# A two-layer graph attention kernel: the sums of W one step later, less background work in three panels, and a bias added by DMA

## The chip, the cores and the metric

The kernel runs on one core of one Trainium2 chip. The metric is the device time of one execution in microseconds (us). Most executions of one kernel lie within 0.3% of each other. Of the kernel before, three runs were known at the start: median 3235.16 us (3231.14 to 3235.99). Every comparison below has its own runs of the kernel before, made on the same chip in the same rounds.

## The reference

There are 2708 rows of 1024 features in float32, and a 0/1 adjacency matrix. Two layers, cut to what matters:

```
# layer 0
h = relu(layernorm(x))
f, g = h @ Wf + bf, h @ Wg + bg
attention = softmax(where(adj > 0, relu(f @ g.T), -9e15), axis=1)
x = x + attention @ (h @ W + bW)
# layer 1
h = relu(layernorm(x)) @ W1
e = leaky_relu(h @ a1 + (h @ a2).T)
x = x + relu(softmax(where(adj > 0, e, -9e15)) @ h)
```

The rows of a softmax sum to one, so `attention @ (h @ W + bW)` is `(attention @ h) @ W + bW`. The kernel uses this form: the bias bW is simply added to the rows of x to which the projected result is added.

## The kernel before

Layer 0 works on five column panels (0 to 4) of the attention matrix, two of 586 columns and three of 512. For each panel there are four stages on TensorE: the scores, the q of the next panel, the aggregate of this panel with h, and the projection with W. All large products are done as seven half-size products, called M1 to M7; the sums that this method needs run on VectorE, GpSimd and ScalarE. Layer 1 follows.

Three parts matter. First, background work. Pieces with an estimated cost in VectorE time are queued, and after a product the code hands out credit for some of them. The loads that a piece needs are issued when it is one of the next two:

```python
def one():
    for it in later[:2]:
        if it[1]:
            it[1]()                    # the loads of this piece
            it[1] = None
    us, _, go = later.pop(0)[:3]
    go()
    return us

def behind(us, psum_free=False):
    credit[0] = min(credit[0] + us, 2 * us)
    while later and credit[0] > 0 and (psum_free or not later[0][3]) and (not later[0][4] or later[0][4]()):
        credit[0] -= one()
```

In the scores, `behind(rate)` follows the products, with `rate = 0.6 if p == 0 else 1.0`. In an aggregate the rate is 3.0.

Second, the sums of the quarters of W (of both layers). `prepare_W` queues eight pieces. Each loads two tiles of 512 KB of W's rows from the stream pool, which has 12 tiles and is shared with `hc`, the rows of h that the aggregate streams in:

```python
def prepare_W():
    def fetch(l, k):
        ...
        rows[l, k] = [load_rows(w_in[l], c, "w_rows") for c in (k, k + NH)]
    def go(l, k):
        two = rows.pop((l, k))
        ...                            # layer 1: dot products with a1, a2
        right_of_W(l, k, *two)         # sums on VectorE, four stores
    for l in range(2):
        for k in range(NH):
            put(2.7 if l == 0 else 8.0, lambda l=l, k=k: go(l, k), lambda l=l, k=k: fetch(l, k))
```

It is called just ahead of the aggregate of panel 0. Third, the rows to which the projection adds:

```python
def finish0(p):
    bwb = [slot(f"bwb{e}") for e in range(2)]
    ...                                # bwb: the bias in every partition
    def start(ts):
        for t in ts:
            ...
            for e in range(2):
                load(xs[t][e], x[r0:r0 + n, e * W:(e + 1) * W])
                nc.gpsimd.tensor_add(xs[t][e], xs[t][e], bwb[e][:n, :W])
```

## Time and profile before

| | kernel before |
|---|---|
| time, median | 3235.16 us |
| span of the profiled run | 3235.3 us |
| TensorE busy | 3137.1 us (97%) |
| TensorE idle (difference) | 98.2 us |
| VectorE busy | 1756.3 us (54%) |
| GpSimd busy | 395.0 us (12%) |
| moved by DMA | 641.43 MB |

How to read it: with TensorE at 97%, the question isn't which engine is the bottleneck. It is where TensorE's 98.2 us of idle time lie, and where its busy time is long because the granted clock is low. The prediction shows the lines for this: the list of TensorE's waits, then the timeline of each stage.

### The profile page before, as it was taken

To read this page: it belongs to the slowest core of one execution; us is meant where nothing else is said; L and a number is where in the kernel's file an instruction comes from. 1 tells how busy PE (TensorE), PEld (TensorE's weight loads), DVE (VectorE), ACT (ScalarE), POOL (GpSimd) and SP (SyncE) were. 2 spreads that over 40 slices of the span, in tenths; PEclk is the share of its full clock that TensorE was granted. 3 is DMA by queue.
4 is the path that set the end of the run, shared out by engine and by line. 5 is a ranking of instruction groups with operands and counts; after the bars stand their busy time and mean duration, and the time that the engine had idled before them with its cause. 6 is when DMAs were issued, how large, how long until landed. Compare 5 with 4: busy or idle time off the path is not lost. (4 is left out here: it accounts for less than half of the span.)

```text
span 3235.3 us, 35363 instructions
## 1 busy us (share of the span) xinstructions
PE 3137.1 (97%) x12924; PEld 2333.4 (72%) x12924; DVE 1756.3 (54%) x3594; ACT 507.7 (16%) x853; POOL 395.0 (12%) x476
## 2 busy tenths in 40 slices
PE   8999999999999999999999998997999999999998
PEld 5577767667876578876888885864767748778585
DVE  7857594275812766327581358537574272553712
ACT  4412120010200102001020002003131030211200
POOL 3723110210002100021000101020010000000001
PEclk9999999999999999999999999998999999999999
DMA  6958866576445575457745565665555445555546
GB/s 262 332 174 297 276 229 227 171 243 215 141 130 163 173 247 190 151 191 242 228 156 156 165 209 185 225 237 200 198 161 175 148 159 171 186 189 175 194 150 212
DMA packets 279628, 641.43 MB, mean 198 GB/s; under 512 B 50686, under 2 KB 116178, under 8 KB 279456
## 3 DMA queue, kind: packets, MB, share of 16 engines
q1 hardware_dynamic: 245184, 525.56, 50.5%
q0 software_dynamic: 34272, 113.62, 9.4%
q8 instruction: 102, 1.67, 0.2%
q14 instruction: 70, 0.57, 0.1%
HBM read 525.49 MB, written 113.58 MB: 198 GB/s over the span
## 5 line engine op out<-in xcount | busy, mean ns | idle before, releaser
L917 PE MATMUL sz<-B,As 128*128 128x256 f32 (+3 forms) x1320 | 328.9, 399 | 5.3 <-DVE st L44 5.3
L917 PEld LDWEIGHTS sz<-B,As 128*128 128x128 f32 (+1 forms) x1320 | 248.7, 189 | 64.5 <-DVE st L44 6.4
L917 PE MATMUL sx<-B,As 128*128 128x256 f32 (+3 forms) x880 | 227.0, 401 | 14.2 <-DMA As<-hs_d 12.0
L756 POOL TENSOR_TENSOR gT<-gT,rr 128x2048 f32<-128x2048 f32 (+3 forms) x20 | 68.3, 3433 | 1320.5 <-DVE rr L44 700.2
L917 PE MATMUL sy<-B,As 128*128 128x256 f32 (+3 forms) x880 | 219.5, 392 | 0.0
L478 PE MATMUL gy<-T,hc 128*128 128x256 f32 (+3 forms) x880 | 205.7, 395 | 6.6 <-DMA hc<-hg_d 6.6
L478 PE MATMUL gx<-P,hc 128*128 128x256 f32 (+3 forms) x880 | 204.5, 394 | 4.7 <-ACT P L1147 4.7
L478 PE MATMUL gz<-Sa,hc 128*128 128x256 f32 (+3 forms) x880 | 206.6, 394 | 0.0
L478 PE MATMUL gz<-P,hc 128*128 128x256 f32 (+3 forms) x880 | 206.3, 393 | 0.0
L917 PEld LDWEIGHTS sx<-B,As 128*128 128x128 f32 (+1 forms) x880 | 162.3, 189 | 51.4 <-issue 11.2
L478 PEld LDWEIGHTS gy<-T,hc 128*128 128x128 f32 (+1 forms) x880 | 168.5, 192 | 42.3 <-DVE junk L44 4.4
L478 PEld LDWEIGHTS gx<-P,hc 128*128 128x128 f32 (+1 forms) x880 | 168.4, 192 | 40.9 <-ACT P L1147 5.0
L917 PEld LDWEIGHTS sy<-B,As 128*128 128x128 f32 (+1 forms) x880 | 163.9, 186 | 38.2 <-issue 0.9
L478 PEld LDWEIGHTS gz<-Sa,hc 128*128 128x128 f32 (+1 forms) x880 | 165.6, 190 | 31.8
L478 PEld LDWEIGHTS gz<-P,hc 128*128 128x128 f32 (+1 forms) x880 | 165.6, 190 | 31.8
L821 PE MATMUL px<-w,gT 128*128 128x512 f32 x320 | 147.3, 613 | 11.5 <-issue 10.0
L821 PE MATMUL py<-w,ps 128*128 128x512 f32 (+1 forms) x352 | 155.6, 593 | 0.3 <-DVE mcol L44 0.3
L821 PE MATMUL pz<-w,ps 128*128 128x512 f32 (+1 forms) x352 | 155.0, 592 | 0.0
L616 ACT COPY mask<-mk_ps 128x1024 bf16<-128x1024 bf16 (+1 forms) x55 | 55.6, 1011 | 575.8 <-PE mk_ps L615 254.6
L821 PEld LDWEIGHTS pz<-w,ps 128*128 128x128 f32 (+1 forms) x352 | 65.5, 186 | 85.6 <-issue 81.7
L821 PEld LDWEIGHTS py<-w,ps 128*128 128x128 f32 (+1 forms) x352 | 65.4, 186 | 85.6 <-issue 82.7
L821 PEld LDWEIGHTS px<-w,gT 128*128 128x128 f32 x320 | 62.5, 197 | 89.2 <-issue 85.3
(240 smaller groups left out, 4797.9 us busy)
## 6 DMA issues: line engine op xcount, KB each, us to landing
hc<-hg_d SPq DMA_DIRECT2D x350, 512.0 KB
As<-hs_d SPq DMA_DIRECT2D x150, 512.0 KB
w<-wt_d SPq DMA_DIRECT2D x96, 512.0 KB
w<-in_L_gnn_W_dram SPq DMA_DIRECT2D x72, 512.0 KB
md<-md_d SPq DMA_DIRECT2D x56, 512.0 KB
adj_i<-in_adj_dram SPq DMA_DIRECT2D x50, 512.0 KB
hg_d<-g POOLq DMA_DIRECT2D x40, 512.0 KB, 5.0
hs_d<-hsT POOLq DMA_DIRECT2D x40, 512.0 KB, 5.6
```

Source lines behind the costliest of these rows:

```text
L478: nc.tensor.matmul(ps[d], left(m, k, d), right(m, k), start=(start and k == 0), stop=(k == K - 1), skip_group_check=True)
L616: nc.scalar.copy(mk[:n, :, :k4 * P], ps[:n, :, :k4 * P])
L756: nc.gpsimd.tensor_tensor(of(e, s), of(e, s), by(s, k), OP.mult)
L821: nc.tensor.matmul(ps, left[i][m][:, k, :], w_[k], start=(start and k == 0), stop=(k == NH - 1), skip_group_check=True)
L917: nc.tensor.matmul(ps[:n, :h], lefts[q][:, i % 2, c, :n], B[m][c // 2][:, c % 2, :h], start=(start and c == 0), stop=(c == NH - 1), skip_g ...
```

## The change

The intent: let the first products of panel 0's aggregate have the load queue for themselves; let VectorE convert the masks in time, by giving panels 2 to 4 fewer credits per product; and take 44 additions from GpSimd, a row of which holds up one VectorE instruction in the kernel before (8.50 us for 0.69).

```diff
-        rate = 0.6 if p == 0 else 1.0
+        rate = (0.6, 1.0, 0.65, 0.65, 0.65)[p]
 ...
     def finish0(p):
-        bwb = [slot(f"bwb{e}") for e in range(2)]
-        for e in range(2):
-            load(bwb[e][:, :W], bass.AP(tensor=bw.tensor, offset=bw.offset + e * W, ap=[[0, P], [1, W]]))
 ...
                     load(xs[t][e], x[r0:r0 + n, e * W:(e + 1) * W])
-                    nc.gpsimd.tensor_add(xs[t][e], xs[t][e], bwb[e][:n, :W])
+                    nc.gpsimd.dma_start(xs[t][e], bass.AP(tensor=bw.tensor, offset=bw.offset + e * W, ap=[[0, n], [1, W]]),
+                                        accum_op=OP.add)
 ...
-        if p == 0:
-            prepare_W()
-        then = {}
+        then = {M5: prepare_W} if p == 0 else {}
```

`then = {M5: prepare_W}` queues the pieces behind the product M5, the second of the aggregate's seven.

## The prediction

> **What bounds the kernel now.** I read the page first, then the list of waits of TensorE, then its timeline stage by stage.
>
> ```profile
> PE 3137.1 (97%) x12924; PEld 2333.4 (72%) x12924; DVE 1756.3 (54%) x3594; ACT 507.7 (16%) x853; POOL 395.0 (12%) x476
> ```
>
> TensorE is busy 97% of 3235.3 us. The change neither adds nor removes a product, so only its idle 98.2 us, and the time in which it runs below full clock, can be won. The list of TensorE's waits says what it is idle for (total, times, longest):
>
> ```profile
> PE mk_ps L615 <- DVE nm L44: 17.0, 9, 3.4
> PE mx_ps L654 <- DVE mx L44: 14.8, 1, 14.8
> PE sx L917 <- DMA As<-hs_d: 12.0, 4, 4.3
> PE px L821 <- issue: 10.0, 3, 4.8
> PE gy L478 <- DMA hc<-hg_d: 6.6, 2, 4.0
> PE sz L917 <- DVE st L44: 5.3, 2, 4.9
> ```
>
> The 14.8 us (column maximum between the layers) and the 10.0 us lie where the last projection of layer 0 waits on VectorE, ScalarE and stores; the change does not move the order of VectorE there. The other rows are its targets. First, the timeline of TensorE in the first aggregate, with one row of the busy-time-by-stretch view below it (columns: stretch, length, busy PE, PEld, DVE, ACT, POOL, granted clock, DMA share, GB/s):
>
> ```profile
> 446.44 21.87 PE L478 MATMUL gx<-Sa,hc 128*128 128x293 f32 x88
> 470.91 6.26 PE L478 MATMUL gy<-T,hc 128*128 128x293 f32 x24 [2.60 <-DMA hc<-hg_d]
> 481.18 18.81 PE L478 MATMUL gy<-T,hc 128*128 128x293 f32 x64 [4.01 <-DMA hc<-hg_d]
> 499.83 21.87 PE L478 MATMUL gx<-Sb,hc 128*128 128x293 f32 x88
> ```
>
> ```profile
> 468.00:490.00 22.00, 15.39 (x51) 10.83 (x50) 20.07 (x56) 0.66 (x2) 6.49 (x12) 0.84 1.02 401
> ```
>
> A product takes 21.7 us start to start when nothing is late (499.83 to 521.54). The second one, gy, should have started at 446.44 + 21.7 = 468.1 and ended 489.8; it ended 499.8. So 10 us are lost: 6.6 idle and some 3 at half clock after the idle time. The DMA engines are full (share 1.02, 401 GB/s): the sums of W's quarters load 16 tiles of 512 KB and store 32 of 256 KB in this stretch, and their loads stand in the one load queue among those of hc.
>
> Second, a narrow panel's scores (panel 3 of 0 to 4), timeline of TensorE:
>
> ```profile
> 1505.02 1.89 PE L917 MATMUL sx<-B,As 128*128 128x256 f32 x8
> 1510.32 0.66 PE L615 MATMUL mk_ps<-identb,nm 128*74 128x128 bf16 x8 [3.42 <-DVE nm L44]
> 1510.80 3.63 PE L917 MATMUL sz<-B,As 128*128 128x256 f32 x8
> 1514.27 1.89 PE L917 MATMUL sy<-B,As 128*128 128x256 f32 x8
> ```
>
> The transposes of the next mask wait 3.42 us for VectorE to convert it, and the product after them takes 3.63 us for 1.89: half clock. Third, the end of panel 4's scores, all engines:
>
> ```profile
> 1942.98 9.81 POOL L1078 TENSOR_TENSOR x_res<-x_res,bwb 128x512 f32<-128x512 f32 x8
> 1944.85 8.50 DVE L44 SCALAR_TENSOR_TENSOR Sb<-Sb,mask 128x512 f32<-128x512 f32 x1
> 1954.46 3.68 PE L917 MATMUL sz<-B,As 128*128 128x256 f32 x8 [4.93 <-DVE st L44]
> ```
>
> One VectorE instruction that takes 0.69 us at 1962.22 takes 8.50 us here, and ends when GpSimd's eight additions of W's bias end. TensorE then idles 4.93 us and runs its next product at half clock.
>
> **What the skill says.** (1) "SBUF — State Buffer", section "Who interferes with whom": a VectorE instruction with two SBUF inputs contends with a GpSimd instruction that reads SBUF, and the loser is blocked, not slowed. The 8.50 us agree, and show that it can stay blocked through a row of GpSimd instructions. (2) "TensorE: Matmul & The Clock Gate", Part 1: after an idle window the array runs at half clock for about 3.4 us, in windows that run freely. The trace agrees: granted clock 0.50 in 1511 to 1514 and 0.51 in 1955 to 1958. So an idle time of 2 us and more costs up to 1.7 us on top, not every time. (3) "DMA: Bandwidth & Descriptors", section "SWDGE vs HWDGE vs iDMA": an accumulating DMA can only be issued from GpSimd; (4) its section "Queues, rings and completion order" has the DMA engines share their time between queues. That nothing but the queue's turn is lost to the accumulate, no run here shows yet.
>
> **The change part by part.** The order of each engine's instructions in the built kernels was compared; no time is in it.
>
> *Sums of the weights later.* Now all 12 loads of hc of the first two products come before any of W's rows, so gx and gy have their data: -10 us. But W's 16 loads and 32 stores move into the third and fourth product. From 490 to 512 (estimated from the new order of the queue) the engines must move 1 MB of rows of a, 2 MB of W's rows, 4 MB of stores and 5 tiles of hc, about 9.5 MB; at the 401 GB/s seen above that is 23.7 us against 21.7. Some loads of hc also reuse a tile of W's rows, which is free only when its sums have been stored; stores took 6.5 us to land here, which is just in time. I take 3 us idle and 1.5 us of half clock: net -5.5.
>
> *Less background per product.* A product of 8 instructions takes 1.73 us; seven make 12.1, and with the mask's transposes a pair of row blocks is 12.6 us. At rate 1.0 the background may take 7 us of VectorE per pair. Summing the VectorE starts-to-starts of the timeline (0.335 us for 256 columns, 0.605 for 512, 0.72 for a dot product's half, 0.62 for a half of the statistics), the early pairs hold 11.8 to 13.5 us in panel 2 and 12.3 to 14.3 in panel 3, against 12.6. At 0.65 they hold 9.0 to 12.7 and 8.1 to 13.1. What decides is the chain from the end of one pair to the conversion of the next mask, which has five products (8.6 us) where the scheduler has put the transposes early: before, it is 8.2 to 10.8 us, with waits of 0.93 to 3.42. After, four early places are left with a chain of 8.0 to 8.8 us: by the same relation about 1 us each; the two short waits at the start of panel 3 (0.72, 1.19) keep their order and stay. Panel 2: 5.2 idle + 1.7 half clock become about 2.1: -4.8. Panel 3: 6.8 + 1.7 become about 4.2: -4.3. Panel 2 also waits 2.84 us for As, with 3 us of half clock (0.50 in 1160 to 1166), after a burst of mask loads for the background in the same queue; they are spread now, and I count half: -3. Panel 4 has no background work left, so its new rate does nothing. The background's queue ends within the scores at the lower rate too: nothing is pushed into a later stage.
>
> *Bias by DMA.* 44 GpSimd additions of 1.257 us each (some 55 us) go, with 10 bias loads; 44 accumulating DMAs of up to 256 KB come, some 11 MB in all against 641. GpSimd is at 12%, so its own time wins nothing. In four of the five projections the additions run under the last product of the aggregate, where VectorE is idle. Only the fifth collides: -4.93 - 1.7 = -6.6. VectorE's order in that projection also changes: it finishes rows earlier and no longer reaches the evictions late, which cost TensorE 2.74 + 0.75 us and about 1 of clock: -4.5.
>
> Sum: -5.5 - 4.8 - 4.3 - 3 - 6.6 - 4.5 = -28.7. Every reordering of such a schedule opens small waits elsewhere (nine mask waits are there now); I allow +5: -24. 3235 - 24 = 3211.
>
> **Rivals.** (a) *The burst only moves.* The third product starves as the second did: for it, the 9.5 MB above and the tiles that wait for stores; against it, a full product of hc is fetched ahead. Then the first part gives 0: 3217. (b) *The accumulate is slow*: it reads and writes SBUF, and its 2 MB fall into a stretch at 320 GB/s (1942 to 1954), so that the rows come late and VectorE, whose new order has them early, blocks the softmax behind them. Against it, 20 us and more lie between issue and use. It would cost 5 to 10: 3219. (c) *VectorE's waits are set by single long pieces*, not by the rate (a pair's sums are 2.7 us at once), so the masks stay late: the second part gives 3 instead of 12: 3220. (d) All three targets vanish and nothing opens: 3199.
>
> **Range and chances.** The gain is bounded by the identified losses, about 40 us or 1.2%, so 2% (65 us) is out of reach, and nothing added is on TensorE. Times before spread from 3231 to 3236. I take 3200 to 3224; faster by over 2% 0.01, within 2% 0.98, slower 0.01.
>
> **What would show it.** Right: no wait of gy for hc; no VectorE mask-add over 2 us in panel 4 and no wait of sz for st there; waits of mk_ps for nm near 10 us instead of 17.0; no POOL addition of bwb; TensorE's idle time near 80 us. Wrong: a wait of gx or gz for hc between 490 and 530 over 5 us, VectorE or the new DMA as releaser of px or pz, or the mask waits unchanged. A loss over 10 us would mean that the accumulating DMAs hold up the queue of loads.

## The result and the profile after

| | before | after |
|---|---|---|
| time, median of 6 runs | 3233.29 us (3231.14 to 3235.99) | 3210.03 us (3208.94 to 3210.75) |
| span of the profiled run | 3235.3 us | 3207.8 us |
| TensorE busy | 3137.1 us | 3125.8 us |
| TensorE idle (difference) | 98.2 us | 82.0 us |

The ratio is 0.9928, with a 95% interval of 0.9915 to 0.9941. A ratio here is the mean time of one kernel's fast runs over the mean of the other's of the same rounds, so it isn't quite the ratio of the two medians. The kernel became faster by 23 us, within 2%. The prediction was 3211. The two profiled runs exaggerate this: that of before is the slowest of its six (3235.99, 2.7 above the median), that of after lies 0.4 below its median. So the spans differ by 27.5 us and the medians by 23.3, and some 4 us of the stage differences below are chance.

From the profile's page of the kernel after, the busy times, and from its list of TensorE's waits (total, times, longest) the rows that answer to those of before:

```profile
PE 3125.8 (97%) x12924; PEld 2326.2 (73%) x12924; DVE 1747.8 (54%) x3593; ACT 508.5 (16%) x853; POOL 381.3 (12%) x476
...
PE mx_ps L654 <- DVE mx L44: 15.1, 1, 15.1
PE sx L917 <- DMA As<-hs_d: 10.6, 3, 6.0
PE px L821 <- issue: 9.8, 3, 4.6
PE mk_ps L615 <- DVE nm L44: 9.5, 8, 2.5
PE gx L478 <- DMA hc<-hg_d: 6.1, 2, 5.8
PE sx L917 <- DVE sm L44: 2.2, 1, 2.2
```

The reader is to see two things. The same 12924 matmul instructions now take 11.3 us less busy time, which can only be clock or overlap, and TensorE is idle 16.2 us less; the two add up to the 27.5 us between the spans. And of the four target rows, one shrank (mk_ps for nm, 17.0 to 9.5), one is nearly gone (sz for st, 5.3 to 0.7), and one merely has another product's name: gy waited 6.6 us for hc, and now gx waits 6.1. The fourth, sx for As, lost its one wait in panel 2 (2.84 us); the three that are left lie in panel 0's scores, which the change doesn't touch.

Where the time went, stage by stage, is read from TensorE's timelines: each stage runs from the start of its first product to the start of the next stage's first.

| stage (us) | before | after | difference |
|---|---|---|---|
| aggregate of panel 0 | 165.31 | 164.68 | -0.6 |
| scores of panel 1 | 163.87 | 162.28 | -1.6 |
| scores of panel 2 | 151.48 | 139.90 | -11.6 |
| scores of panel 3 | 147.25 | 143.96 | -3.3 |
| scores of panel 4 | 144.82 | 137.94 | -6.9 |
| projection behind it | 55.04 | 48.94 | -6.1 |
| from the last product to the end | 11.02 | 12.86 | +1.8 |

The time up to the aggregate of panel 0 (446.44 and 446.81 us) and each other stage agree within 0.4 us. Up to its last product TensorE thus gained 29.3 us, and the tail took 1.8 back. A stage of unchanged code doesn't take the same time in every execution, so each difference needs that spread beside it. In the traces of this case that lack the change's part for a stage, the aggregate of panel 0 took 164.1 to 166.4 us, the scores of panel 1 163.8 to 165.5, of panel 2 147.1 to 151.5, of panel 3 145.5 to 148.6, of panel 4 144.8 to 146.2, and the projection behind it 53.3 to 55.0. The kernel after lies below all of these ranges except the first.

The aggregate of panel 0 in the kernel after: the timeline of TensorE, then two stretches of the busy-time view (columns as in the prediction):

```profile
446.81 21.87 PE L478 MATMUL gx<-Sa,hc 128*128 128x293 f32 x88
468.52 21.88 PE L478 MATMUL gy<-T,hc 128*128 128x293 f32 x88
490.24 13.98 PE L478 MATMUL gx<-Sb,hc 128*128 128x293 f32 x56
510.03 6.92 PE L478 MATMUL gx<-Sb,hc 128*128 128x293 f32 x16 [5.81 <-DMA hc<-hg_d]
521.27 21.87 PE L478 MATMUL gz<-Sa,hc 128*128 128x293 f32 x88
```

```profile
446.80:490.20 43.40, 43.40 (x177) 33.42 (x176) 19.27 (x45) 2.96 (x6) 0.00 (x0) 1.00 0.47 149
490.20:521.30 31.10, 25.01 (x90) 18.24 (x89) 23.26 (x55) 1.13 (x3) 10.80 (x20) 0.89 0.97 365
```

The first two products are whole now, at full clock and with the DMA engines half used. The third takes 521.27 - 490.24 = 31.0 us instead of 21.7: the full engines, the wait of 5.8 us and the lowered clock (0.89) have moved with the burst by one product.

Panel 3's scores, at the pair that waited 3.42 us before:

```profile
1498.23 0.61 PE L615 MATMUL mk_ps<-identb,nm 128*74 128x128 bf16 x8
1498.67 1.90 PE L917 MATMUL sx<-B,As 128*74 128x256 f32 x8
```

The transposes start without a wait, and the product behind them takes 1.90 us, not 3.63.

The end of panel 4's scores, all engines, and of the view of the accumulating DMAs' line two rows (durations in ns min/median/max, then landing times in us):

```profile
1926.77 6.17 POOL L1075 DMA_DIRECT2D x_res<-in_L_gnn_bW_dram  x7 [0.53 <-DVE sm L44]
1928.13 0.69 DVE L44 SCALAR_TENSOR_TENSOR Sb<-Sb,mask 128x512 f32<-128x512 f32 x1
1936.10 1.89 PE L917 MATMUL sz<-B,As 128*128 128x256 f32 x8
```

```profile
L1075 POOL DMA_DIRECT2D x_res<-in_L_gnn_bW_dram x44: 819/1872/3292, 597.1 to 2114.2; - x44
DMA to landing us min/median/max: 6.3/13.4/21.1
```

The mask addition on VectorE that took 8.50 us takes 0.69 while GpSimd issues the DMAs; sz follows without a wait at full clock. Seven issues take 6.17 us, 0.88 us each. The median of 1.872 us in the second fence isn't the cost of one: the records of neighbouring issues overlap, and the line's busy time is 38.9 us for all 44. Between 1900 and 2010 us TensorE waits for nothing at all, where it waited for st, pt and mcol before (4.9, 2.7 and 0.5 + 0.3 us).

### The profile page after: what moved, and what is told of

Read it like the earlier page. It is cut to its first block, busy times and chain, and to the rows that moved or that the text cites. A ratio compares the mean times of both kernels' runs of the same rounds, so it can differ in the third digit from the quotient of the medians.

```text
span 3207.8 us, 35361 instructions
## 1 busy us (share of the span) xinstructions
PE 3125.8 (97%) x12924; PEld 2326.2 (73%) x12924; DVE 1747.8 (54%) x3593; ACT 508.5 (16%) x853; POOL 381.3 (12%) x476
## 4 chain that ended last, share of the span: by engine, by line
PE 82%; issue 9%; DVE 3%; DMA 3%; POOL 2%; ACT 1%; SPq 0%; POOLq 0%; DVEq 0%; ACTq 0%
PE gy L478 13%; PE gz L478 12%; PE gx L478 12%; PE sz L917 8%; PE sx L917 5%; PE sy L917 5%; PE pz L821 4%; PE M_ps L413 3%; PE qz L478 3%; PE gv L478 3%; PE py L821 3%; PE px L821 3%; PE qy L478 2%; PE qx L478 2%; DMA As<-hs_d 1%
## 5 line engine op out<-in xcount | busy, mean ns | idle before, releaser
L917 PE MATMUL sz<-B,As 128*128 128x256 f32 (+3 forms) x1320 | 321.4, 392 | 0.7 <-DVE st L44 0.7
L478 PEld LDWEIGHTS gz<-Sa,hc 128*128 128x128 f32 (+1 forms) x880 | 165.5, 190 | 31.9
L478 PEld LDWEIGHTS gz<-P,hc 128*128 128x128 f32 (+1 forms) x880 | 165.5, 190 | 31.9
L821 PE MATMUL px<-w,gT 128*128 128x512 f32 x320 | 147.6, 614 | 11.3 <-issue 9.8
```

Source lines behind the costliest of these rows:

```text
L478: nc.tensor.matmul(ps[d], left(m, k, d), right(m, k), start=(start and k == 0), stop=(k == K - 1), skip_group_check=True)
L821: nc.tensor.matmul(ps, left[i][m][:, k, :], w_[k], start=(start and k == 0), stop=(k == NH - 1), skip_group_check=True)
L917: nc.tensor.matmul(ps[:n, :h], lefts[q][:, i % 2, c, :n], B[m][c // 2][:, c % 2, :h], start=(start and c == 0), stop=(c == NH - 1), skip_g ...
```

## The experiments

The kernel before, in the runs of the first four experiments: median 3234.15 us (17 runs). The theory was that each of the three parts acts in its own stages: the sums almost not at all, since the burst only moves; the rates in panels 2 and 3; the bias only in the projection behind panel 4. The main rival was that the bias DMA, by freeing GpSimd and the SBUF access, is what helps the masks too.

### e1_sums: the sums alone

```diff
-        if p == 0:
-            prepare_W()
-        then = {}
+        then = {M5: prepare_W} if p == 0 else {}
```

> The kernel before with only the sums of W queued later. In the trace of the changed kernel the second product of the first aggregate no longer waits for hc, but the third waits 5.8 us instead and runs at half clock after it, so the aggregate as a whole is 0.6 us shorter. Theory (the burst only moved): 0 to -2 us against before, no wait of gy, a wait of gx for hc of 5 to 6 us. Rival (my prediction's step: most of the burst is absorbed by the product fetched ahead, and what the changed kernel shows there comes from the other parts): -5 us or more, wait under 3 us.

Measured: 3231.5 us median of 13 runs, ratio 0.9993 (0.9984 to 1.0001); one of them took 3683.91 us at a granted clock of 0.845; it was slow and is left out of the ratio. The aggregate took 163.61 us, 1.7 less than before, and the third product waits in the place of the second. From TensorE's timeline of this run:

```profile
489.44 13.98 PE L478 MATMUL gx<-Sb,hc 128*128 128x293 f32 x56
508.23 6.87 PE L478 MATMUL gx<-Sb,hc 128*128 128x293 f32 x16 [4.81 <-DMA hc<-hg_d]
```

What follows: rival (a) of the prediction, the burst that only moves, is what happens; the part alone is worth 2.3 us by the ratio, with an interval from 5.2 us down to nothing. Its aggregate, 163.61 us, is only 0.5 us under the fastest one of unchanged code (164.06 in e5_twice).

### e2_rates: the rates alone

```diff
-        rate = 0.6 if p == 0 else 1.0
+        rate = (0.6, 1.0, 0.65, 0.65, 0.65)[p]
```

> The kernel before with only the lower rates in panels 2 to 4. Theory (VectorE's background work between products delays the masks and bursts of mask loads delay As): panel 2's scores 11 to 12 us shorter, panel 3's about 3, panel 4's end unchanged with its 8.5 us mask-add, together -13 to -16 us. Rival (panel 2 got its time from GpSimd and buffers freed by the bias part): panel 2 gains under 6 us, total over -9.

Measured: 3222.58 us median of 5 runs (one, 4378.32 us at a granted clock of 0.705, is slow and left out of the ratio), ratio 0.9962 (0.9949 to 0.9976): 11.6 us by the medians, a little less than the 13 to 16 expected. Panel 2's scores took 139.90 us, the same as with all parts, and panel 3's 145.35. The row mk_ps for nm fell to 9.0 us in 8 waits. Panel 4's scores and the projection behind it stayed at 146.16 and 53.33. What follows: the masks' waits and the wait for As in panel 2 are the rate's, with the bias's additions still there. The six traces with the old rate all have a wait for As in panel 2 (1.5 to 4.0 us), and the seven with the new rate have none. That panel 4's rate has no part in it needs no run: a build of the changed kernel with 1.0 there gives the same program, byte for byte.

### e3_bias: the bias by DMA alone

```diff
-        bwb = [slot(f"bwb{e}") for e in range(2)]
-        ...
-                    nc.gpsimd.tensor_add(xs[t][e], xs[t][e], bwb[e][:n, :W])
+                    nc.gpsimd.dma_start(xs[t][e], bass.AP(tensor=bw.tensor, offset=bw.offset + e * W, ap=[[0, n], [1, W]]),
+                                        accum_op=OP.add)
```

> The kernel before with only the bias added by the DMA. Theory (the lock between GpSimd's additions and VectorE's mask-add at the end of panel 4, and the later order of VectorE there): -11 to -14 us, all of it between the start of panel 4's scores and the end of the projection behind them. Rival (GpSimd's and the buffers' time helps everywhere): gains spread over several projections and scores, or over 16 us. If accumulating DMAs cost the path anything, a new wait of px, py or pz shows it.

Measured: 3219.59 us median of 5 runs (3218.79 to 3220.97), ratio 0.9955 (0.9941 to 0.9968). Panel 4's scores took 137.94 us and the projection 48.94, together 13.0 less than before, exactly as with all parts. By the medians the run gained 14.6 us, 0.6 more than expected. mk_ps for nm stayed at 17.0 us in 9 waits. Panel 2 took 147.12 here against 151.48, but executions whose code for panel 2 is unchanged spread from 147.1 to 151.5, so this isn't the bias's.

### e4_bias_p3: the bias by DMA in one projection

The DMA is used only in the projection behind panel 4's scores; the other four keep GpSimd's additions.

```diff
+        if p != NP - 2:
             bwb = ...
 ...
+                    if p != NP - 2:
                         nc.gpsimd.tensor_add(xs[t][e], xs[t][e], bwb[e][:n, :W])
+                    else:
+                        nc.gpsimd.dma_start(xs[t][e], ..., accum_op=OP.add)
```

> Bias by DMA only in the projection that runs behind panel 4's scores, by GpSimd as before in the other four. Theory (only this one collides): the same time as the run with all five by DMA, within 2 us. Rival (every projection gains a little): less than half of that run's gain.

Measured: 3221.95 us median of 5 runs (3217.97 to 3226.52), ratio 0.9961 (0.9948 to 0.9973). Panel 4 and the projection took the same 137.94 and 48.94 us. What follows: eight of the 44 additions are nearly the whole gain. The median is 2.4 us above that of e3, slightly more than expected, but the intervals overlap, so the times show nothing for the other 36. The traces show one thing: panel 1's first product still waits 1.57 us for VectorE here, and in e3_bias, as in the kernel after, that wait is gone (see the allowance below).

### e5_twice: eight more additions behind the eight

If GpSimd's row of additions shuts VectorE out to its end, a row twice as long should shut it out twice as long. In the kernel before, in that one projection, each half row has the bias added twice (the result is wrong only if bW isn't zero, which it is here).

```diff
                     nc.gpsimd.tensor_add(xs[t][e], xs[t][e], bwb[e][:n, :W])
+                    if p == NP - 2:
+                        nc.gpsimd.tensor_add(xs[t][e], xs[t][e], bwb[e][:n, :W])
```

> The kernel before, but in the projection behind panel 4's scores GpSimd adds the bias twice (the bias is zero in these inputs, so the result stays right). Theory (VectorE's mask-add is shut out until GpSimd's row of additions ends): the mask-add that took 8.5 us takes 16 to 19 us, sz waits 13 to 15 us for st, and panel 4's scores grow by 8 to 10 us over the kernel before. Rival (one long VectorE instruction for another reason, such as a late mask or the profiler): the mask-add stays near 8.5 us and the stage grows by under 2 us.

Measured: one run of 3232.7 us, state unknown. Both expectations fell. From the timeline, VectorE and GpSimd:

```profile
1942.65 1.27 POOL L1080 TENSOR_TENSOR x_res<-x_res,bwb 128x512 f32<-128x512 f32 x1
1943.16 1.31 DVE L44 SCALAR_TENSOR_TENSOR Sb<-Sb,mask 128x512 f32<-128x512 f32 x1
1943.88 1.72 POOL L1078 TENSOR_TENSOR x_res<-x_res,bwb 128x512 f32<-128x512 f32 x1
```

The mask addition waited only for the end of the GpSimd instruction that was running (1943.92), then ran its free 0.69 us less some start-up, to 1944.47; the next GpSimd instruction was the one held up (1.72 us for 1.25). Panel 4's scores took 137.94 us, as good as with the DMA. The projection became slower, 57.13 us, where a wait of pz for pt is 4.8 us at the longest. So a longer row isn't a longer lock. My explanation at this point was that the second additions depend on the first ones and so leave gaps in the row.

### e10_row: four more additions that depend on nothing

This tests that explanation: four additions into scratch tiles among the eight, none waiting for a neighbour. (Made in the last batch; the kernel before there: median 3233.45 us of 7 runs.)

```diff
+            if p == NP - 2:
+                for i in range(4):
+                    nc.gpsimd.tensor_add(slot(f"scr{i}")[:, :W], bwb[0][:, :W], bwb[1][:, :W])
```

> The kernel before, with four more GpSimd additions of 128x512 among the eight of W's bias in the projection behind panel 4. Unlike in the run with the additions done twice, they depend on none of their neighbours, so the row of some twelve should have no gap, 12 x 1.23 = 14.7 us. If VectorE is shut out for a whole gap-free row, its mask addition in that stretch takes 8.5 + 4.9 = 13 to 14 us (0.69 free), TensorE waits about 10 us for st behind it, and panel 4's scores take 149 to 151 us against 144.8 before. If it was something else that let VectorE in there (where in the row its instruction comes to stand, or a bound on the time it is held), the mask addition stays at or below 8.5 us and the scores at or below 145. Whichever half-clock stretch follows may add or take 1.7 us.

Measured: one run of 3220.03 us, state unknown. Panel 4's scores took 138.28 us: the second expectation, at or below 145. From the timeline, GpSimd and VectorE:

```profile
1937.87 4.95 POOL L1078 TENSOR_TENSOR x_res<-x_res,bwb 128x512 f32<-128x512 f32 x4
1939.74 3.64 DVE L44 SCALAR_TENSOR_TENSOR Sb<-Sb,mask 128x512 f32<-128x512 f32 x1
1943.46 1.78 POOL L1081 TENSOR_TENSOR scr<-bwb,bwb 128x512 f32<-128x512 f32 x1 [0.64 <-DVE Sb L44]
1948.78 0.71 DVE L44 SCALAR_TENSOR_TENSOR Sa<-Sa,mask 128x512 f32<-128x512 f32 x1
1948.89 1.75 POOL L1081 TENSOR_TENSOR scr<-bwb,bwb 128x512 f32<-128x512 f32 x1
```

The row did not become twelve long: a scratch tile was late, and GpSimd paused 0.64 us after its fourth addition. The mask addition had been held past two boundaries between additions (it started in the second of the four), and it ended at 1943.38, 0.56 us after the row's end (1942.82). In the kernel before it ended at 1953.35, again 0.56 us after the row's end (1952.79); in e5_twice, 0.55 us after the end of one instruction. So what shuts VectorE out is GpSimd: in all three places the mask addition ends 0.55 to 0.56 us after a GpSimd addition does. But in this same run, after the pause, VectorE got in between additions that follow each other without a pause (1948.78), as in e5_twice. Gaps from dependences are therefore not the whole rule, and what decides at which boundary VectorE gets in stays open.

### e6_slots, e7_slow, e8_slots_slow: why the third product starves

Three explanations of what is left in panel 0's aggregate: W's rows hold stream tiles that hc needs; the burst is too dense for the DMA engines; or both. The kernel before in these runs: median 3232.07 us (9 runs). All three start from the changed kernel. e6_slots puts W's rows into tiles of another pool, as halves; e7_slow lowers the background rate in that aggregate alone; e8_slots_slow does both.

```diff
 # e6_slots
-            rows[l, k] = [load_rows(w_in[l], c, "w_rows") for c in (k, k + NH)]
+            rows[l, k] = [row_halves("w_rows", P) for _ in range(2)]
+            ...                        # four loads of half rows
 # e7_slow
-        G[p] = aggregate(0, p, S, got["sm"], then)
+        G[p] = aggregate(0, p, S, got["sm"], then, rate=2.0 if p == 0 else 3.0)
```

> The changed kernel with W's rows in the other pool of buffers (as halves of 512 columns), so that no load of hc reuses a tile of W's rows. Theory (the third product waits because its tile is held until the sums of W are stored): the wait of gx for hc goes under 1.5 us and the first aggregate falls from 164.7 us to 155 to 158. Rival (the DMA engines are simply full there): a wait of 4 us or more stays, aggregate over 161.

Measured: 3216.64 us median of 5 runs (3216.01 to 3220.55), ratio 0.9954 (0.9942 to 0.9967): worse than the changed kernel, with the aggregate at 173.47 us. From the load queue's timeline and, in the second fence, TensorE's waits:

```profile
452.11 47.73 SPq L121 DMA_DIRECT2D w_rows<-in_L_gnn_W_dram  x16
499.89 3.15 SPq L121 DMA_DIRECT2D hc<-hg_d  x2
```

```profile
PE gx L478 <- DMA hc<-hg_d: 15.6, 3, 12.7
```

Sixteen loads of W's rows stood at the head of the queue for 47.73 us, waiting for tiles of the other pool, and hc, whose tiles were free, stood behind them. The experiment did not separate what it was made for: the new pool had no room either, and it showed the order of the queue instead.

> The changed kernel with 2.0 instead of 3.0 us of background work per step in the first aggregate alone, tiles as in the changed kernel: the same bytes over more products. Theory (tile held): the first sums still run at once after the second product, so the third product still waits 3 us or more; aggregate 161 to 165. Rival (engines full): the burst is thinner and the wait falls under 1.5 us; aggregate 155 to 158.

Measured: 3207.04 us median of 4 runs (3205.1 to 3207.37), ratio 0.992 (0.9907 to 0.9934). The aggregate took 161.48 us, 3.2 less than in the changed kernel. From TensorE's timeline:

```profile
491.01 21.87 PE L478 MATMUL gx<-Sb,hc 128*128 128x293 f32 x88
517.16 23.58 PE L478 MATMUL gz<-Sa,hc 128*128 128x293 f32 x88 [4.27 <-DMA hc<-hg_d]
```

The third product is whole now, and the fourth waits 4.27 us. The burst is thinner but still ends in one wait. Neither expectation came whole: the third product's wait is gone, as the rival said, but the aggregate isn't at 155 to 158 us.

> Both edits together on the changed kernel: W's rows in the other pool and 2.0 us per step. Theory and rival both: no wait of gx, gy or gz for hc, first aggregate at 155 to 156.5 us, 8 to 10 us under the changed kernel's time, some 3201 us.

Measured: 3216.13 us median of 5 runs (3213.05 to 3221.55), ratio 0.9952 (0.9938 to 0.9965), aggregate 170.88 us. Twelve loads of W's rows stand at the head of the queue for 37.50 us here, so the other pool's tiles hold it up at the lower rate as well. The expectation (no wait, some 3201 us) failed: the third product waits 5.80 us.

### e9_q: W's rows from another queue

The cleaner test of the queue: the tiles stay, the loads of W's rows are issued by GpSimd.

```diff
-            rows[l, k] = [load_rows(w_in[l], c, "w_rows") for c in (k, k + NH)]
+            rows[l, k] = [stream("w_rows") for _ in range(2)]
+            for c, t in zip((k, k + NH), rows[l, k]):
+                nc.gpsimd.dma_start(t, w_in[l][c * P:(c + 1) * P, :])
```

> The changed kernel, with the sixteen loads of W's rows issued from GpSimd's queue instead of the load queue; tiles, sums and rates as they are. Three explanations of the 5.8 us that the third product still waits for hc. (1) Order in the load queue: loads of hc stand behind loads of W's rows that wait for a tile. Then the wait of gx for hc falls below 1.5 us, the first aggregate takes 159 to 161.5 us start to start against 164.7, and the time is 3 to 5 us under the changed kernel's 3210. (2) The DMA engines are full whichever queue the bytes come from: the wait stays at 4 to 6 us, the aggregate at 163 to 166, the time within 1.5 us of 3210. (3) The tiles themselves are short, hc takes the buffers that W's rows hold: the wait stays or grows, and the load queue shows hc itself waiting for a product or a store.

Measured: 3209.86 us median of 4 runs (3209.62 to 3210.01), ratio 0.993 (0.9915 to 0.9945). The third product still waits, 4.40 us (5.81 before), and the aggregate takes 161.73 us. But now hc itself waits for its tile, and for what it waits is a store of the sums of W. The load queue's own waits, 440 to 545 us:

```profile
SPq L121 <- DMA wt_d<-w_rows: 38.1, 6, 14.9
SPq L121 <- PE gy L478: 36.8, 2, 33.2
```

Of the three expectations this is the third, that the tiles are short: a tile that W's rows took comes back to hc only when its sums have been stored. One load of hc waited 33.2 us (to 488.1) for a tile of the second product, since W's rows had taken the eight that came free before; another waited 7.9 us (to 506.3) for a store, just ahead of the third product's wait (509.8 to 514.2). The longest wait for a store, 14.9 us, ended at 525 us and cost TensorE nothing. The aggregate is 3.0 us shorter than the changed kernel's, as the second expectation did not allow (163 to 166), while the time is that of the changed kernel: in this profiled run the stages up to the aggregate took 448.41 us against 446.81, and other stages some tenths more.

### e11_rates: a version meant to beat both

The changed kernel with the rate of e7_slow, and 0.75 and 0.55 as the rates of panels 1 and 3.

```diff
-        rate = (0.6, 1.0, 0.65, 0.65, 0.65)[p]
+        rate = (0.6, 0.75, 0.65, 0.55, 0.65)[p]
```

> A version meant to beat both: the changed kernel with background rate 2.0 in the first aggregate (it measured 3207.0) and the rates of panels 1 and 3 lowered too, to 0.75 and 0.55. If what is left in panels 1 and 3 is VectorE's conversions coming late behind background pieces, their scores go from 162.3 to 159.5-161 and from 144 to 141-143, and the time is 3 to 5 us under 3207. If the remaining waits are set by the long single pieces or by the start of the panel (the wait of the first product for VectorE), nothing moves: 3206 to 3208. Work pushed out of panel 1's scores into the next projection could cost 1 to 3 us there.

Measured: 3206.43 us median of 4 runs (3205.08 to 3207.36), ratio 0.992 (0.9904 to 0.9937). All four runs lie under the fastest of the changed kernel (3208.94; the kernel before was alike in the two batches, 3233.29 and 3233.45), so it looks some 3 us faster than the changed kernel, though the intervals of the two ratios overlap; against e7_slow (3207.04) nothing is shown. Panel 1's scores took 162.17 us, as in the changed kernel (162.28): its two waits for masks (3.5 us) are gone, and its first product waits 2.1 us for VectorE instead. Panel 3's took 142.82 (143.96), with 1.7 us left for masks and 2.5 for VectorE at the start. This is the second expectation: the lower rate takes the mask waits away, and most of it comes back as a wait at the panel's start.

## Why the prediction was right

The time was right (3211 against 3210.03), but its three parts were not all right: the sums of W gave 4 to 5 us less than counted, and of the allowance of 5 us for new waits less than half was needed. That these errors cancelled to 1 us is luck.

**Sums of the weights later: wrong.** The prediction counted -5.5. Measured are -0.6 in the changed kernel and -1.7 in e1_sums, hardly more than the spread of this stage. The step that failed is "I take 3 us idle and 1.5 us of half clock" for the third product: it lost 521.27 - 490.24 - 21.7 = 9.3 us, 5.8 + 0.3 of it idle. The estimate that 9.5 MB would need 23.7 us against 21.7 counted the DMA engines alone. e9_q shows the term that was taken as "just in time": with the loads of W in their own queue, a load of hc still waited 7.9 us for a tile that a store had to free. In the changed kernel itself the load queue's longest such wait is 6.5 us, and there are twelve, 28.6 us in all (440 to 540 us). The longest ends at 501.24 us; it is one of W's rows, with the next load of hc right behind it (501.66). The stores that I had counted at 6.5 us take 8.6 us to land at the median here. The engines are full at the same time (share 0.97), and how much of the wait is theirs isn't separated. e7_slow and e11_rates show that thinning the burst wins back 3.2 us (161.48 and 161.44). Rival (a) had the outcome for this part.

**Less background per product: right in kind, with one term mis-sized in panel 2.** The prediction had -4.8 and -3 in panel 2 and -4.3 in panel 3; measured are -11.6 and -3.3. In panel 2 the waits for masks went from 5.2 us in three to 1.1 us in two, and the 1.7 us of half clock behind them went too; with a new wait of 0.3 us that is -5.5. The wait for As (2.84 us) with the half clock after it (3 us) went altogether, -5.8, where I "count half". That term was mis-sized for this execution. e2_rates alone gives the same 139.90 us, so nothing else is in it. But against all executions of unchanged code (147.1 to 151.5) panel 2 gained 7.2 to 11.6 us, and the -7.8 predicted lies within: in e3_bias and e10_row the wait for As is 1.5 and 2.0 us and no half clock follows it. In panel 3 three waits of 1.5 us and less remain, and a wait of the first product for sm grew from 0.7 to 2.2 us: a part of the allowance for new small waits. That panel spreads by 3 us too, mostly by whether half clock follows its wait of 3.42 us (147.25 us with it, 145.50 without it in e3_bias). Panel 4's rate does nothing, as said.

**Bias by DMA: right.** The prediction had -6.6 for the lock at the end of panel 4 and -4.5 for VectorE's order in the projection; measured are -6.9 and -6.1. The second term was not too small by as much as that looks: in e1_sums and e2_rates the unchanged projection takes 53.3 us, because no half clock follows its wait of 2.7 us there, and against them the gain is 4.4. e4_bias_p3 confirms "Only the fifth collides" as far as the lock goes. The mechanism as I read it, blocked "through a row of GpSimd instructions", is what the kernel before shows; e5_twice and e10_row show that a row of additions does not always do it. The collision is a matter of where the instructions fall, and the DMA takes the possibility away.

**The allowance of +5.** TensorE gained 29.3 us where the sum said 28.7, but some 4 us of that come from the slow profiled run of before. What came back is 1.8 us in the tail, the 1.5 us at panel 3's start (already in its -3.3) and differences below 0.5 us elsewhere. Panel 1, whose rate is unchanged, won 1.6 us: the wait of its first product for sm (1.50 us before) is gone. It is gone in all traces that have the bias by DMA in every projection and the old rate in panel 1, and it is there in the others. In e3_bias, e6_slots and e8_slots_slow panel 1 takes 163.8 us or more all the same, because half clock follows the mask wait of 2.49 us there (granted clock 0.55 from 687.7 to 691.4 us of e3_bias, 1.00 at that place in the kernel after). The way it works, as far as the traces show: GpSimd issues the store of a row at 660.16 us, not at 662.94, and ScalarE, which overwrites the row, waits for the store 0.86 us, not 2.33. The prediction gave the other four projections nothing. The tail was not in the prediction. It is 11.0 to 11.7 us in the five executions whose code has no accumulating DMA (before, e1, e2, e5, e10) and 11.9 to 13.1 in the others; the difference lies behind the issue of the last store (4.91 us to the end before, 6.75 after), and what makes it longer is open.

**Half clock.** Much of the spread comes from it, and the thirteen traces bear out the prediction's "2 us and more" and "not every time". Of TensorE's waits between 640 and 2135 us, none of the 93 up to 1.57 us lowered the granted clock of the next 3.2 us (one of 0.30 us lies in the slow stretch behind a longer wait); of the 45 between 2.0 and 3.43 us, 22 did (to 0.50 to 0.72); of the five from 4.0 us up, all did. But 1.7 us is not the most that it costs: behind the wait for As the clock was 0.50 for 6 us, which is 3 us, as the prediction itself shows.

**The rivals.** (b), a slow accumulate, has a true premise: a landing takes 13.4 us at the median, against 3.7 for GpSimd's plain stores of x in the kernel before. It stayed harmless, because VectorE waits for none of these rows between 1930 and 1990 us: the first is issued at 1926.77 us and used at 1948.77. (c), long single pieces, is refuted by e2_rates. (d), that everything vanishes, failed by the part of the sums; its 3199 isn't worked out, and the losses that the prediction lists add up to some 42 us, which would be 3193.

**The signs.** The prediction named a wait of gx for hc over 5 us as a sign against it; that came (5.8). The sign for the masks (near 10 us: 9.5), for panel 4 (no mask addition over 2 us) and the idle time (near 80 us: 82.0) came too. VectorE is still the releaser of pz in three waits of 0.8 us, which would be a sign against it, but the same three are in the kernel before.

## What to carry to other kernels

Moving a burst of transfers to a later place won next to nothing here, where the later place has the same deadline and the same buffers; thin it out, and count the buffers with the time until a store frees them, not only the bytes against the engines. When one engine's instruction takes many times its normal duration and ends with another engine's row, look for sharing between the two and move the work that is off the path to where it can't collide, here a DMA whose rows are used some 20 us after the issue. Before reading a stage's difference as an effect, look at how far that stage spreads in runs of unchanged code, here by up to 4.4 us. And when a prediction of several parts comes out right as a sum, run each part alone before believing the parts.

## What the Trainium skill lacked or had wrong

- "SBUF — State Buffer", section "Who interferes with whom": it says, of VectorE's two-port modes, that who issues first has the shared port pair for the whole instruction; of an instruction with two SBUF inputs, as the mask addition is, it says only that it contends. In e5_twice the first rule fits (the mask addition waited for one instruction, 1.31 us in all). In the kernel before VectorE's instruction started in the second of GpSimd's eight additions and was held through the other six (8.50 us for 0.69), and in e10_row through two more (3.64 us), although those started later than it. The page doesn't say at which boundary the waiting engine gets its turn, and the runs don't settle it.
- "DMA: Bandwidth & Descriptors", section "SWDGE vs HWDGE vs iDMA": it names GpSimd as the only issuer of accumulating DMAs, but gives no cost for the accumulate. Here 44 of them, of up to 256 KB each, kept GpSimd busy for 38.9 us, 0.88 us each, against 0.55 for a plain store of the same half row and 1.23 for the addition that each replaces (54.0 us for 44). They took 13.4 us to land at the median (6.3 to 21.1), against 3.7 for the stores of x in the kernel before.
- The same page has no figure for what a load costs whose buffer isn't free: on the load queue sixteen such loads held everything behind them for 47.73 us in all (e6_slots), loads with free buffers too.
- "TensorE: Matmul & The Clock Gate", Part 1, has no figure for how often an idle time of 2 to 3.4 us is followed by half clock. Here 22 of 45 waits between 2.0 and 3.43 us were, and none of 93 shorter ones by itself.
